# Last three products of the first pair's first conditional layer taken at two levels, and the fourth mW1 unit expanded later

## The chip, the cores and the metric

The kernel runs on one core of one Trainium2 chip. The metric is device microseconds of one execution. Before the change the median of three runs is 1162.1 us (1162.05, 1162.10 and 1163.01). All times below are microseconds from the start of the profiled execution's span unless they are said to be durations.

## What is computed

Four sequences of 512 tokens by 512 channels pass an attention with a projection, then two feed-forward networks, then a small adapter:

```
attn_out = softmax(x Wq (x Wk)^T * scale) x Wv Wp + bp
cms      = gelu(attn_out cW1 + cb1) cW2 + cb2 + one_hot(code)
modifier = gelu([attn_out, cms] mW1 + mb1) mW2 + mb2
y        = clip(x + cms + modifier, 0, 1)
out      = layernorm(y + gelu(y Wdown[s] + bd) Wup[s] + bu) * g + b
```

cW1 is 512 x 2048, cW2 2048 x 512, mW1 1024 x 2048, mW2 2048 x 512; everything is float32. The change lies in the first line of the feed-forward part, `gelu(attn_out cW1 + cb1)`, and in the preparation of mW1.

## The kernel before

**Pairs and layers.** The four sequences are worked on as two pairs; in a pair one sequence gives the left and the other the right column block of the right-hand operand. After the attention of both pairs, the loop over pairs runs five stages: `c1_layer` (cW1 and gelu), `second_layer` with cW2 (called c2 below), `m1_layer` (mW1 and gelu), `second_layer` with mW2 (m2), and the adapter, which for the first pair is spread over the second pair's c1.

**Seven products for eight, at one or two levels.** Every layer is a Strassen-Winograd product: seven block products numbered 1 to 7 stand for eight. In c2, m1 and m2 each of the seven is again cut into seven (two levels). In c1 of the second pair all seven products are at two levels (`c1_two_level`). In c1 of the first pair only products 1 and 5 are; products 2, 6, 7, 3 and 4 are plain products of 128x512 matmuls (L1327). The order is `FIRST_C = (2, 1, 5, 6, 7, 3, 4)`.

**What a two-level product of c1 needs.** It needs the four sums of its weight block (five to eight in the weight tile, operands of inner products 5, 6, 7 and 3) and the four sums of its token block. The weight sums of products 6, 7, 3 and 4 (`C1_BESIDE`) are made on GpSimd in the weight tile itself (L1229: 8 instructions of 128x256 for a product, for two weight tiles). The token sums are made by `inner_sums` (L1168 on): by VectorE, or on GpSimd with four 128x256 instructions (L1176 to L1179). `seven` runs the inner products in the order 1, 5, 6, 2, 7, 3, 4: the first uses unsummed blocks, the second needs the first weight sum and the first token sum. When product 6 or 7 is at two levels, its results are added into the hidden blocks partly by GpSimd (L1267: eight 128x512 additions for a product).

**Weight tiles.** Four tiles `wslot` are used in turn, two for a product, loaded by SP in a fixed order (`fetch`). A product's tiles come free when the product two before it has ended.

**Expansion.** Ahead of c2, m1 and m2 the weights are expanded on GpSimd: `expand` takes one unit (256 columns or rows of each block), makes seven sets of sums and writes them to DRAM (`m1_kept` and so on), from where SP loads them as they are needed. `expansion` is a generator: two units of cW1, two of cW2, then the four units of mW1. `steps` advances it between pieces of the attention and after each piece of the first pair's c1. A unit first issues its sums, three plain sets, the raw load of the next unit (`then`, four DMAs at L381), three full sets, and last the `fourth` set, which is written into the tiles `first` and `part`. `late_expansion` does the same for the two units of mW2 during m1, in the tiles `mod`, `slot[0]`, `slot[6:8]`.

**What sets the order.** The order in which each engine issues its instructions is fixed when the program is built: a planner goes by program order among the instructions that it believes ready at its own estimate of the time. `tc.keep_in_program_order(i)` pins an instruction behind the one traced before it on its engine. Once built, an engine takes its queue strictly in order: one that waits holds up all behind it.

**The step into c2.** `second_operands` prepares the operands of c2 and m2 from the hidden blocks: `operands(0)` are the four sums of the block `h22` for the first product of the second layer (product 3 in `SECOND`), `differences` the outer operands, and `after(p, g)` is called when a part of c1 or m1 is done. For the first pair's c1 (`busy`) VectorE makes `operands(0)` and half of two differences while product 4 runs; for the second pair's c1 GpSimd makes `operands(0)`, and half of the first difference is made by a scaled copy on ScalarE (L1448) and an adding DMA (L1455).

Of the kernel before, what the change touches and what calls it, by code (L numbers as in the profile page):

```python
# [18 lines left out]
def kernel(  # L19
# [121 lines left out]
    def flat(t):  # L141
        return t.rearrange("p c n -> p (c n)")
# [117 lines left out]
    C1_PLAIN = {1: (0, 0), 2: (1, 0), 4: (1, 1)}  # L260
    C1_SUM = {3: 2, 6: 0, 7: 1}
    C1_BESIDE = (6, 7, 3, 4)
    C1_KEPT = (2,)

    c1_outer = [spill.tile([P, 3, 2, 2, 256], F32, name=f"c1_outer{u}") for u in range(2)]
# [188 lines left out]
    def expansion():  # L454

        c2_units = [(cW2, False, c2_kept, u) for u in range(2)]
        yield from expand_c1(0, lambda: load_c1(1, nc.gpsimd))
        yield from expand_c1(1, lambda: load_raw(cW2, False, 0, slot[4:6]))

        constants()  # L460
        yield from expand_all(
            c2_units + m1_units, slot[4:6], (flat(part), slot[3], slot[1]), flat(first)
        )

    def late_expansion():

        spaces = (flat(mod[0]), flat(mod[1]), slot[0])
        quarters = lambda tiles: [t[:, at : at + 1024] for t in tiles for at in (0, 1024)]
        begin, rest = expand_c1_late(quarters(slot[6:8]), quarters(spaces[:2]))
        yield from expand_all(m2_units, slot[6:8], spaces, None, begin)  # L470
        yield from rest

    def inner_weights(src, is_first, store, p, u):

# [685 lines left out]
    def c1_operands(slots=(0, 1, 2, 3)):  # L1160


        at0, at1, t12, t34 = (in_rows[i] for i in slots)
        b11, b12, b21, b22 = at0[:, 0:2, :], at1[:, 0:2, :], at0[:, 2:4, :], at1[:, 2:4, :]
        t1, t2, t3, t4 = t12[:, 0:2, :], t12[:, 2:4, :], t34[:, 0:2, :], t34[:, 2:4, :]
        operands = {1: b11, 2: b21, 3: b22, 4: t4, 5: t1, 6: t2, 7: t3}

        def inner_sums(p, k, eng=None):  # L1168

            s = mod[1][:, 2 * k : 2 * k + 2, :].rearrange("p a (b n) -> p (a b) n", b=2)  # L1170
            t = operands[p]
            s1, s2, s3, s4 = (s[:, i : i + 1, :] for i in range(4))
            if eng is None:
                return inner_operands(t, 1, [s1, s2, s3, s4], pinned=True)
            c11, c12, c21, c22 = t[:, :1, :256], t[:, :1, 256:], t[:, 1:, :256], t[:, 1:, 256:]
            eng.tensor_tensor(s1, c12, c11, ALU.subtract)  # L1176
            eng.tensor_tensor(s2, c22, s1, ALU.subtract)
            eng.tensor_tensor(s3, c22, c12, ALU.subtract)
            eng.tensor_tensor(s4, c21, s2, ALU.subtract)  # L1179
            return {1: c11, 2: c21, 3: c22, 4: s4, 5: s1, 6: s2, 7: s3}  # L1180

        def minus(out_, one, two):
            tc.keep_in_program_order(nc.vector.tensor_tensor(out_, one, two, ALU.subtract))

        minus(t1, b12, b11)

        def rest():
            minus(t2, b22, t1)
            yield
            minus(t3, b22, b12)  # L1190
            minus(t4, b21, t2)
            yield

        return operands, inner_sums, rest()
# [2 lines left out]

        tc.keep_in_program_order(nc.sync.dma_start(out=out, in_=in_))

    def c1_two_level(p, h, rhs, after, beside):  # L1200


        a = []
# [64 lines left out]
            if p == 7 and place in ((0, 1), (1, 0)):  # L1268
                gelu(h[3], 1, cb1_c, (first_tile, first_tile + 1))

        then = {6: [beside], 7: [beside], 4: [beside]} if beside is not None and p != 2 else {}
        if p == 4:

            then[2] = [lambda: after(p, 0)]

        copy = nc.vector.tensor_copy if p in (3, 4) else nc.scalar.copy
        seven(2, matmuls, keep, (1, 5, 6, 2, 7, 3, 4), then, copy, at=mod[0])
        if p == 5:
            gelu(h[0], 0, cb1_c, range(8))
        elif p == 6 and 3 in C1_BESIDE:  # L1280
            after(3, 0)
        elif p in (3, 4):
            after(p, 1)

    def c1_layer(h, rhs, after, more, beside):

        operands, inner_sums, rest = rhs
        two = [p for p in FIRST_C if p in ((2, 1, 5, 6, 7, 3, 4) if more else (1, 5))]
        ready = {}

        def prepare(i):
# [5 lines left out]
        for p in FIRST_C:  # L1297
            if p in two:
                if more or p == 1:
                    prepare(two.index(p) + 1)  # L1300
                c1_two_level(p, h, ready[p], after, beside if more else None)
                if more:
                    next(rest, None)
                yield
                continue
            for g in range(2):
# [27 lines left out]
                        combine_first_tile(p, h, 4 * g + t, ps, cb1_c)  # L1334
                if p == 2:
                    next(rest, None)
                after(p, g)
                if more:
                    beside()
                yield  # L1340

    def combine_first_tile(p, h, t, ps, bias_c):
        h11, h12, h21, h22 = (b[:, t, :] for b in h)
        if p == 6:
            add(ps, ps, h21)
            add(h12, ps, h22)
            nc.scalar.copy(h21, ps)
        elif p == 7:
            add(ps, ps, h21)
            add(h22, ps, h22)  # L1350
            nc.scalar.copy(h21, ps)
            gelu(h[3], 1, bias_c, (t,))
        else:
            i, half = {3: (1, 0), 4: (2, 1)}[p]
            dst = h[i][:, t, :]
            add(dst, ps, dst)
            gelu(h[i], half, bias_c, (t,))

    def m1_operands():

# [56 lines left out]

    LOW, HIGH = slice(0, 4), slice(4, 8)

    def second_operands(h, busy=False, eng=None):  # L1420

# [17 lines left out]
        def after(p, g):  # L1441

            if (p, g) == (3, 1) and eng is not None:
                ready.append(operands(0, eng))
            if (p, g) == (3, 0) and not busy:
                for two in (slice(0, 2), slice(2, 4)):
                    tc.keep_in_program_order(
                        nc.scalar.activation(t1[:, two, :], h11[:, two, :], AF.Copy, scale=-1.0)  # L1448
                    )
            elif (p, g) == (3, 1):  # L1450
                if busy:
                    differences(1, LOW)
                    differences(3, LOW)
                else:
                    nc.gpsimd.dma_start(out=t1[:, LOW, :], in_=h12[:, LOW, :], accum_op=ALU.add)  # L1455
            elif (p, g) == (4, 0) and eng is None:
                ready.append(operands(0))
            elif (p, g) == (4, 1):
                differences(1, HIGH)

        def begin():
            if not busy:
                differences(3, LOW)

        ready = []
        return operands, differences, after, ready, begin

    def second_layer(made, src, kept_w, c, last, bias_c, beside):

        operands, differences, _, ready, begin = made  # L1470
        c11, c12, c21, c22 = c
# [1 line left out]
        for i, p in enumerate(SECOND):  # L1473
# [19 lines left out]
            def matmuls(q, ps):  # L1493
# [14 lines left out]
            inner(  # L1508
                matmuls, [[v[:, o, t, :] for t in range(2)] for o in range(2)], 256,
                None if half is None or bias_c is None else bias_c[:, half : half + 2],  # L1510
                first if bias_c is not None else mod[0],
            )
            if p == 6:
                z6 = z
# [217 lines left out]
    for pair in range(B // 2):  # L1732
        final = pair == B // 2 - 1

        h = next_hidden()
        made = second_operands(h, pair == 0, nc.gpsimd if final else None)
        between = expanding if pair == 0 else extra
        for _ in c1_layer(h, c1_rhs, made[2], final, lambda: steps(extra, 1)):
            if not final:
# [4 lines left out]
        m1_made = m1_operands()  # L1744
        m1_rhs = []

        def beside_c2(i, pair=pair):
            if i == 4:

                load_attn(pair)  # L1750
            elif i == 6:
                m1_rhs.append(m1_made(0))

        for _ in second_layer(made, cW2, c2_kept, blocks_of(cms), c_last(pair), None, beside_c2):
            pass

        h = next_hidden()
        made = second_operands(h)
# [118 lines left out]
```

## Time and profile before

| | |
|---|---|
| median of 3 runs | 1162.1 us |
| profiled execution: its own time | 1163.66 us |
| its span, first to last instruction | 1162.0 us |
| granted TensorE clock | 0.999 |
| PE / DVE / ACT / POOL busy | 99% / 77% / 25% / 46% of the span |
| first pair: c1 | 237.43 to 330.27 |
| first pair: c2 | 330.27 to 415.08 |
| first pair: m1 | 415.08 to 585.37 |
| first pair: m2 | 585.37 to 669.98 |

PE is TensorE, DVE VectorE, ACT ScalarE, POOL GpSimd, SP the queue that issues the weight loads. A line of the timeline view gives start, duration, engine, source line, operation, output and input, and in brackets how long the engine sat idle before it and what ended that wait. The chain of waits names the work that led to the end of the program, followed back step by step.

### The profile page before, as it was taken

The numbers are of one execution on the slowest core, as the hardware profiler recorded it, in microseconds if no ns is written. First come the engines' busy times: TensorE is split into PE (matmuls) and PEld (weight loads), VectorE is DVE, ScalarE is ACT, GpSimd is POOL, SyncE is SP. The second block draws the span as 40 slices with busy tenths as digits, with TensorE's granted clock in tenths as the row PEclk, the third lists the DMA queues.
The fourth block names the chain that finished last, engine by engine and source line by source line (L and its number), as shares of the span: only waits on it lengthen the run. The fifth ranks groups of instructions, "written<-read, shape, count | busy, mean of one in ns | idle before, by whom it ended". The sixth has DMA issues, their size and how long they took to land.

```text
span 1162.0 us, 13643 instructions
## 1 busy us (share of the span) xinstructions
PE 1153.4 (99%) x4941; PEld 922.6 (79%) x4941; DVE 892.2 (77%) x1227; ACT 293.5 (25%) x535; POOL 532.4 (46%) x611
## 2 busy tenths in 40 slices
PE   9999999999999999999999999999999999999997
PEld 8588468556478888888888877778888888888875
DVE  5755755487699965899699956789994588689955
ACT  4244426235520000013310036372000003230014
POOL 4999989888950068795200317971000001120001
PEclk9999999999999999999999999999999999999999
DMA  9695594898676578888837742145745364585601
GB/s 278 252 268 188 190 399 172 320 368 289 263 271 239 182 249 317 321 285 334 263 130 305 224 158 91 65 161 197 267 156 188 146 240 158 177 304 193 230 3 72
DMA packets 100482, 258.87 MB, mean 223 GB/s; under 512 B 23554, under 2 KB 58688, under 8 KB 85184
## 3 DMA queue, kind: packets, MB, share of 16 engines
q1 hardware_dynamic: 77088, 157.17, 38.5%
q0 software_dynamic: 19888, 89.17, 21.6%
q10 hardware_dynamic: 3440, 11.67, 2.6%
q8 instruction: 39, 0.64, 0.2%
q14 instruction: 27, 0.22, 0.1%
HBM read 188.78 MB, written 66.06 MB: 219 GB/s over the span
## 4 chain that ended last, share of the span: by engine, by line
PE 97%; DVE 2%; issue 1%; DVEq 0%
PE i L1495 29%; PE i L1395 27%; PE sum L756 10%; PE sum L1237 9%; PE sum L690 8%; PE c L1327 6%; PE down_ps L1587 2%; PE up_ps L1606 2%; PE tr_ps L522 1%; DVE hidden L600 1%; PE up_ps L1601 1%; DVE slot L252 1%; DVE part L1099 0%; PE tr_ps L943 0%; PE idle_ps L237 0%
## 5 line engine op out<-in xcount | busy, mean ns | idle before, releaser
L1395 PE MATMUL i<-slot,wslot 128*128 128x256 f32 x1184 | 261.4, 379 | 0.6 <-DVE part L1099 0.6
L1395 PEld LDWEIGHTS i<-slot,wslot 128*128 128x128 f32 x1184 | 224.6, 190 | 32.1 <-DVE part L1099 1.3
L1495 PE MATMUL i<-slot,wslot 128*128 128x256 f32 x896 | 202.7, 379 | 0.0
L1495 PEld LDWEIGHTS i<-slot,wslot 128*128 128x128 f32 x896 | 170.2, 190 | 23.4 <-DVE cms L1099 0.3
L1495 PE MATMUL i<-hidden,wslot 128*128 128x256 f32 x576 | 132.1, 379 | 0.0
L1495 PEld LDWEIGHTS i<-hidden,wslot 128*128 128x128 f32 x576 | 109.4, 190 | 15.7 <-issue 0.7
L1099 DVE TENSOR_TENSOR part<-i,part 128x512 f32<-128x512 f32 (+1 forms) x156 | 90.5, 591 | 34.0 <-PE i L1395 24.6
L1106 ACT COPY first<-i 128x512 f32<-128x512 f32 (+1 forms) x42 | 21.6, 514 | 375.7 <-PE i L1395 220.9
L1128 ACT ACTIVATE hidden<-hidden,bias 128x512 f32<-128x512 f32 x128 | 83.9, 716 | 87.3 <-DVE hidden L600 77.3
L1763 POOL DMA_DIRECT2D slot<-xT_kept x4 | 2.8, 706 | 152.9 <-PE i L1395 152.9
L1237 PE MATMUL sum<-mod,wslot 128*128 128x256 f32 x288 | 66.6, 379 | 0.0
L252 DVE TENSOR_TENSOR slot<-hidden 128x1024 f32<-128x1024 f32 x46 | 61.4, 1334 | 0.0
L1237 PEld LDWEIGHTS sum<-mod,wslot 128*128 128x128 f32 x288 | 54.7, 190 | 7.4
L1766 POOL TENSOR_TENSOR cms<-cms,slot 128x512 f32<-128x512 f32 x16 | 26.0, 1650 | 73.2 <-PE i L1395 42.6
L252 DVE TENSOR_TENSOR slot<-hidden,slot 128x1024 f32<-128x1024 f32 x46 | 56.7, 1234 | 0.3
L1327 PE MATMUL c<-slot,wslot 128*128 128x512 f32 x128 | 55.3, 592 | 0.0
L1099 DVE TENSOR_TENSOR part<-i,first 128x512 f32<-128x512 f32 (+1 forms) x50 | 31.4, 632 | 29.4 <-PE i L1395 18.5
L600 DVE TENSOR_TENSOR sum<-sum,wslot 128x512 f32<-128x512 f32 x48 | 33.2, 696 | 26.3 <-PE sum L756 18.6
L600 DVE TENSOR_TENSOR hidden<-part,hidden 128x2048 f32<-128x2048 f32 x20 | 52.9, 2646 | 0.5
L756 PE MATMUL sum<-hidden,wslot 128*128 128x256 f32 x232 | 53.2, 379 | 0.0
L381 POOL DMA_DIRECT2D slot<-in_L_cond_mW x24 | 17.9, 752 | 73.3 <-DVE slot L252 72.3
L1327 PEld LDWEIGHTS c<-slot,wslot 128*128 128x128 f32 x128 | 24.3, 190 | 30.6 <-issue 27.7
(344 smaller groups left out, 2097.1 us busy)
## 6 DMA issues: line engine op xcount, KB each, us to landing
wslot<-m_kept SPq DMA_DIRECT2D x48, 1024.0 KB, 6.4
wslot<-m_kept SPq DMA_DIRECT2D x36, 512.0 KB, 4.5
wslot<-c_kept SPq DMA_DIRECT2D x16, 1024.0 KB, 6.3
slot<-in_L_cond_mW POOLq DMA_DIRECT2D x24, 512.0 KB, 7.4
wslot<-in_L_cond_mW SPq DMA_DIRECT2D x24, 512.0 KB, 6.3
wslot<-in_L_cond_cW SPq DMA_DIRECT2D x40, 256.0 KB, 5.0
slot<-in_L_cond_cW POOLq DMA_DIRECT2D x12, 512.0 KB, 6.2
m_kept<-wide POOLq DMA_DIRECT2D x6, 1024.0 KB, 7.5
```

The lines of the kernel that those rows point to most:

```text
L252: i = eng.tensor_tensor(out_, one, two, ALU.subtract)
L600: nc.vector.tensor_tensor(dst, a, b, ALU.add)
L690: nc.tensor.matmul(ps, lhsT=lhs[p][:, c, r * P : (r + 1) * P], rhs=rhs[p][:, c, :], start=(first_ and c == 0), stop=(c == 1), skip_group_c ...
L756: nc.tensor.matmul(v[:, j, :], lhsT=lhs[p][:, c, j * P : (j + 1) * P], rhs=rhs[p][:, c, :], start=(first_ and j == 0 and c == 0), stop=(c ...
L1099: nc.vector.tensor_tensor(dst, ps, other, ALU.add)
L1128: nc.scalar.activation(block[:, t, :], block[:, t, :], AF.Gelu, bias=bias_c[:, 8 * half + t : 8 * half + t + 1],)
L1237: nc.tensor.matmul(halves_of(ps)[:, j, :], lhsT=a[g][:, at_[q], j * P : (j + 1) * P], rhs=rhs[q][:, 0, :], start=(first_ and j == 0), stop ...
L1327: nc.tensor.matmul(ps, lhsT=lhs(c, t), rhs=operands[p][:, c, :], start=(c == 0), stop=(c == 1),)
L1395: nc.tensor.matmul(out_ps[:, j, :], lhsT=a[j][q][:, c, :], rhs=now[q][:, c, :], start=(c == 0), stop=(c == 1),)
L1495: nc.tensor.matmul(ps[:, :256], lhsT=a[k // 2][q][:, k % 2, :], rhs=now[q][:, k, :], start=(k == 0), stop=(k == 3),)
L1587: nc.tensor.matmul(ps, lhsT=wd[:, c, n * P : (n + 1) * P], rhs=y[:, c, tokens], start=(c == 0), stop=(c == NV - 1),)
L1766: nc.gpsimd.tensor_tensor(cms[s][:, d, :], cms[s][:, d, :], in_rows[3][:, d, :], ALU.add)
```

## The change

- In the first pair's c1, products 7, 3 and 4 also go through `c1_two_level` (`C1_TWO`). Their weight sums come on GpSimd, as those of the second pair do.
- Their token sums are made on GpSimd, all twelve instructions pinned one behind the other, traced right behind product 5. The ones of 7 and 3 lie in `mod[1]`, those of 4 in `first`.
- `expansion` ends with the third unit of mW1. The fourth is made by `expand_in_place` in two parts: its raw load is issued at the second product of c2 into `mod`; one set (of block a11) is made at the seventh product of c2 in the tile of `h[2]`; all others follow when c2 is done, in the tiles of `h[2]` and `h[0]`, and a11, a21 and a12 are overwritten by their own sums.
- The first pair's step into c2 is made as the second pair's: `operands(0)` on GpSimd, half of the first difference by ScalarE and an adding DMA, half of the third at c2's start. The call `after(3, 0)` comes behind product 7 for the first pair.
- The first pair's c2 uses `first` in place of `mod[0]` for its intermediate.

```diff
+    AHEAD = (7, 6)
+    C1_TWO = ((1, 5, 7, 3, 4), (2, 1, 5, 6, 7, 3, 4))
...
-            c2_units + m1_units, slot[4:6], (flat(part), slot[3], slot[1]), flat(first)
+            c2_units + m1_units[:3], slot[4:6], (flat(part), slot[3], slot[1]), flat(first)
...
+    def expand_in_place(space, later):
+        u = 3
+        load_raw(mW1, True, u, [flat(t) for t in mod])
+        yield
...
+        def keep(p, a, to, sums_too=True):
+            inner_sums(a, to)
+            at = m1_kept[p, u]
+            if sums_too:
+                nc.gpsimd.dma_start(out=block(at[:, :1024]), in_=a)
+                at = at[:, 1024:]
+            nc.gpsimd.dma_start(out=at, in_=to)
+
+        keep(1, a11, spaces[0], False)
+        yield
+        s1 = block(spaces[4])
+        nc.gpsimd.tensor_tensor(s1, a21, a22, ALU.add)
+        inner_sums(s1, spaces[5])
+        nc.gpsimd.dma_start(out=m1_kept[5, u], in_=later[:, :2048])
+        nc.gpsimd.tensor_tensor(a21, a11, a21, ALU.subtract)
+        nc.gpsimd.tensor_tensor(a11, s1, a11, ALU.subtract)
+        keep(6, a11, spaces[6])
+        keep(7, a21, spaces[7])
+        keep(2, a12, spaces[1], False)
+        nc.gpsimd.tensor_tensor(a12, a12, a11, ALU.subtract)
+        keep(3, a12, spaces[2])
+        keep(4, a22, spaces[3], False)
+        yield
...
-        def inner_sums(p, k, eng=None):
-            s = mod[1][:, 2 * k : 2 * k + 2, :].rearrange("p a (b n) -> p (a b) n", b=2)
+        def inner_sums(p, k, eng=None, fixed=False):
+            space = first if k == 2 else mod[1][:, 2 * k : 2 * k + 2, :]
+            s = space.rearrange("p a (b n) -> p (a b) n", b=2)
...
+            for out_, one, two in ((s1, c12, c11), (s2, c22, s1), (s3, c22, c12), (s4, c21, s2)):
+                i = eng.tensor_tensor(out_, one, two, ALU.subtract)
+                if fixed:
+                    tc.keep_in_program_order(i)
...
-        two = [p for p in FIRST_C if p in ((2, 1, 5, 6, 7, 3, 4) if more else (1, 5))]
+        two = [p for p in FIRST_C if p in C1_TWO[more]]
...
+                c1_two_level(p, h, ready[p], after, then)
+                if p == 5 and not more:
+                    for k, later in enumerate((7, 3, 4)):
+                        ready[later] = inner_sums(later, k, nc.gpsimd, True)
+                if p == AHEAD[more]:
+                    after(3, 0)
...
-        made = second_operands(h, pair == 0, nc.gpsimd if final else None)
+        made = second_operands(h, nc.gpsimd)
...
+        last_unit = iter(()) if final else expand_in_place(flat(h[2]), flat(h[0]))
+
+        def beside_c2(i, pair=pair, last_unit=last_unit):
+            if i in (1, 6):
+                next(last_unit, None)
...
-        for _ in second_layer(made, cW2, c2_kept, blocks_of(cms), c_last(pair), None, beside_c2):
+        for _ in second_layer(
+            made, cW2, c2_kept, blocks_of(cms), c_last(pair), None, beside_c2,
+            mod[0] if final else first,
+        ):
             pass
+        next(last_unit, None)
```

## The prediction

> **What bounds the kernel.** I read the page's first part, the chain of waits, the busy time by stage over the first pair's c1, and then GpSimd's timeline there.
>
> ```profile
> PE 1153.4 (99%) x4941; PEld 922.6 (79%) x4941; DVE 892.2 (77%) x1227; ACT 293.5 (25%) x535; POOL 532.4 (46%) x611
> ...
> 237.43 13.73 PE c L1327 x32
> 251.16 24.17 PE sum L1237 x112
> 275.34 54.93 PE c L1327 x128
> 330.27 84.81 PE i L1495 x392
> 415.08 60.45 PE i L1395 x280
> ```
>
> TensorE never rests, and through c1 the chain is TensorE alone. So a matmul that goes is time that goes, and a wait that comes is time that comes. The fourth line is products 6, 7, 3 and 4, plain: 54.93 / 4 = 13.73 each. The third is products 1 and 5 at two levels: 24.17 / 2 = 12.09 each.
>
> ```profile
> 275.30:289.10 13.80, 13.80 (x34) 6.14 (x33) 10.45 (x15) 4.81 (x9) 9.63 (x15) 1.00 1.02 361
> 289.10:302.80 13.70, 13.70 (x33) 6.05 (x32) 11.12 (x16) 8.33 (x15) 12.25 (x12) 1.00 0.84 334
> 302.80:316.50 13.70, 13.70 (x34) 6.05 (x33) 6.23 (x9) 7.26 (x11) 13.63 (x19) 1.00 0.63 230
> 316.50:330.30 13.80, 13.80 (x34) 6.14 (x33) 13.72 (x10) 3.62 (x6) 13.73 (x15) 1.00 0.78 295
> ```
>
> One line is one product (6, 7, 3, 4); the columns are stretch and length, then PE, PEld, DVE, ACT and POOL (each with its count), clock, DMA share, GB/s. POOL is what to look at: GpSimd, which is to make the new sums, is already full here, with units three and four of mW1.
>
> ```profile
> 272.51 3.01 POOL L381 DMA_DIRECT2D slot<-in_L_cond_mW  x4
> ...
> 279.63 0.57 POOL L398 DMA_DIRECT2D m_kept<-part  x1
> ...
> 284.25 0.73 POOL L247 TENSOR_TENSOR slot<-slot 128x256 f32<-128x256 f32 x1
> 290.52 0.73 POOL L242 TENSOR_TENSOR part<-first 128x256 f32<-128x256 f32 x1 [5.54 <-DMA m_kept<-part]
> ...
> 294.94 2.38 POOL L395 TENSOR_TENSOR part<-slot,slot 128x1024 f32<-128x1024 f32 x1
> ```
>
> Here unit three ends: the raw load for unit four, the full sets up to 284.98, a wait until the store of `part` has landed, the fourth set, and at 294.94 unit four begins.
>
> **What goes.** Three products at 13.73 - 12.09 = 1.64 us: 4.9 us of TensorE, all on the path. Product 7 still begins at 289.0, since nothing ahead of it changes on TensorE.
>
> **When GpSimd gets to the new work.** The token sums are pinned behind unit three, so its end counts. The raw load (3.01) goes, so the full sets end at 281.97 and the store of `part` is issued at 276.6. Before, it took 10.9 us from issue to its release (279.63 to 290.5), with 2 MB of raw load ahead; the same store issued at 197.74 had landed by 203.07, at most 5.3 us. I take 6, nearer the second row since the load is gone: landing at 282.6. The fourth set lasts 4.4 us (290.52 to 294.92), so unit three ends at 287.0; with the two rows as bounds, 286.4 to 291.9.
>
> [...]
>
> **What GpSimd then has to do.** Prices come from the second pair's c1, where all of these exist:
>
> ```profile
> 741.74 5.77 POOL L1229 TENSOR_TENSOR wslot<-wslot 128x256 f32<-128x256 f32 x8
> ...
> 752.11 4.95 POOL L1267 TENSOR_TENSOR hidden<-hidden,hidden 128x512 f32<-128x512 f32 x4
> ...
> 778.21 2.38 POOL L252 TENSOR_TENSOR slot<-hidden 128x1024 f32<-128x1024 f32 x1
> ```
>
> Weight sums: 5.77 for a product. Additions of product 7: 4.95 / 4 = 1.24, eight are 9.9. `operands(0)`: starts 2.33 apart, four are 9.7 (with their last one's tail). Token sums: 128x256 instructions start 0.69 apart in unit three, twelve are 8.3. Together 3 x 5.77 + 9.9 + 9.7 + 8.3 = 45.2 us, beginning at 287.0; the three products and c2's first product want it by about 330. The second pair has 115.7 us for its c1 (669.98 to 785.68), with adapters in between; here four products have some 50.
>
> **Product 7.** Inner product 1 runs to 289.0 + 1.73 = 290.7. Inner product 5 needs the first weight sum. Those sums stand behind the twelve token sums in program order, and the token sums are ready at once when unit three ends. So I put the weight sums behind all twelve: 287.0 + 8.3 = 295.3, the first done at 296.0. Wait: 5.3 us. After that each later weight sum comes 1.4 us apart for a pair and inner products last 1.73, so nothing more. Bounds: nothing, if the planner slots the weight sums between or ahead of the token sums (their tiles are loaded by about 283); 10.2, if unit three ends at 291.9.
>
> [...]
>
> **Products 3 and 4.** Product 7 ends at 289.0 + 12.09 + 5.3 = 306.4. GpSimd: weight sums of 7 to 301.1, of 3 (tiles free since 289.0) to 306.8. Product 3 needs the first at 308.1: no wait. The additions follow to 316.7. Then `operands(0)`, traced ahead of product 4's weight sums, competes with them. Its third and fourth sums overwrite `slot[7]`, which product 3 still reads, so I put two of the four first (4.7), then the weight sums: the first done at 322.1. Product 4 starts at 318.5 and needs it at 320.2: 1.9 us. Bounds: nothing, if the weight sums go first; 6.9, if all four go first (316.7 + 9.7 + 0.7 - 320.2). c1 ends at 318.5 + 12.09 + 1.9 = 332.5, 2.2 later than the 330.27 of before. The last sums of `operands(0)` end near 332, and c2's inner product 7 needs the third at 332.5 + 5.2: covered.
>
> **VectorE, ScalarE and SP.** Product 7 costs VectorE 16 instructions of 0.69 as before (two by eight tiles). Products 3 and 4 rise from 8 to 18 of 0.65 to 0.70, some 12 of 12.09 us: covered, but barely. The pieces that leave it (`operands(0)`, 325.46 to 334.42, and the 3.76 at 317.18) come off the same stretch. In the second pair, with the same work, c2 took 84.61 (785.68 to 870.29), so I carry 0, up to 1 us if the cover fails. SP loads the same bytes; c2's first tiles come free at product 3's end and the loads take 6.3, a product ahead.
>
> **The fourth unit.** Four raw issues (3.01) and one set (2.8 and 0.57) fall in c2, where GpSimd is idle from 334.5 to 406.7 and VectorE busy 11.9 of 12.1; one set cannot cost more than its 3.4, and I take nothing. After c2 there follow 4 x 2.35 + 24 x 0.69 + 9 x 0.57 = 31 us, and behind that the mW2 expansion: it reuses `mod`, so it starts near 447 and not 410.95, and ends near 560 (533.70 before, its first 10 us of raw waits gone). Its first stores for m2 fall at some 545, against m2's start at 585: in time. Behind it queue the xT load and the cms additions (7.8 and 7.1: until 575) and the adding DMA of L1455 (9.2 to landing: 585), wanted some 12 us into m2. In time. What I do charge: in 487.6 to 512.2 VectorE is busy 24.32 of 24.6 and TensorE loses 0.6, with VectorE's 128x512 sums stretched from 0.68 to 3.31 beside GpSimd. The overlap moves into 536 to 585, where VectorE has 20 and 19 of 24.4. First pair's m1 is 170.29, the second's 169.37, so at most 0.9 can be won; I take 1.0 lost, bounds -0.9 and 3.
>
> **Sum.** -4.9 + 5.3 + 1.9 + 0 + 1.0 = +3.3 (the 0.1 is rounding of 4.93). The profiled execution was 1163.66 with a span of 1162.0, so 1.6 above the median of 1162.1; I add the difference to the median: **1165.3 us**.
>
> **Rivals.**
> 1. *The weight sums come early* (faster). The planner issues product 7's weight sums before or between the token sums. For it: in the second pair GpSimd's weight and token sums are interleaved (703 to 713). Against it: there each token sum waited for its space, here nothing holds them. Product 7 then waits 0 to 1, product 4 nothing to 1.9: -4.9 + 0.5 + 0.5 + 0.8 = -3.1, 1159.0. It decides when the first weight sum is done before 293.3, which leaves a wait of 2.6 in all.
> 2. *GpSimd's lateness and the saving cancel*: unit three ends at 286.4 (wait 4.7), product 4's weight sums go first, m1 as before: -0.2 to +2, near 1162.8.
> 3. *`operands(0)` as a whole ahead of product 4's sums*, and unit three nearer its late bound: waits 7.5 and 6.9, +10.5, 1172.
> 4. *The saving is not there*, as two-level products need VectorE for 18 instructions: +1 a product. It is within the others' range.
>
> **Chances.** Forecast (two waits, 1164.5 to 1168.5) 0.40; rival 1 0.22; rival 2 0.23; rival 3 0.15. Faster by over 0.2% (2.3 us, about what a measurement of this kernel can tell from no change) is rival 1: 0.22. Within 0.2%: rival 2 and no more, 0.23. Slower: 0.55. Range: 1159.2 to 1171, which leaves out half of rival 1 and the worst of 3; the likeliest case's own is 1164.5 to 1168.5.
>
> **What would show it.** L1237 in place of L1327 for products 7, 3 and 4, 12.1 us each but for waits; a TensorE wait near 290.7 that a GpSimd L1229 ends, of 5 us; a second near 320; unit three's end near 287; m1's length against 170.29. Wrong if the first L1229 comes ahead of the pinned token sums, or if the largest wait lies with VectorE or in m2.

## The result, and the profile after

The changed kernel takes **1177.8 us** (median of four runs, 1175.74 to 1179.21), against 1162.55 for the kernel before on the same chip: a ratio of 1.0129, with a 95% interval of 1.011 to 1.0149. It is slower, and above the range of the prediction.

The profiled execution took 1179.05 us, its span 1177.3, so 15.3 more than the 1162.0 of before. By the starts of each stage's first matmul in TensorE's timeline, the first pair's stages went so: c1 from 92.84 to 97.32, c2 from 84.81 to 85.58, m1 from 170.29 to 180.97, m2 84.60 and 84.61. The rest of the kernel gave 0.6 back. So m1, whose own products the change leaves as they were, lost most.

First the page's line of busy time, then the stretches of products 6, 7, 3 and 4 (columns as in the prediction):

```profile
PE 1153.3 (98%) x5013; PEld 938.5 (80%) x5013; DVE 911.5 (77%) x1242; ACT 291.8 (25%) x531; POOL 582.1 (49%) x662
```

```profile
275.10:288.75 13.65, 13.65 (x34) 6.00 (x33) 10.44 (x15) 4.68 (x8) 12.18 (x19) 1.00 0.97 379
288.75:310.26 21.51, 15.22 (x58) 12.18 (x56) 9.64 (x15) 2.25 (x4) 21.04 (x29) 0.84 0.19 66
310.26:322.35 12.09, 12.09 (x58) 10.64 (x57) 11.35 (x19) 5.64 (x9) 10.57 (x10) 1.00 0.22 66
322.35:334.43 12.08, 12.08 (x57) 10.64 (x56) 11.27 (x19) 7.74 (x13) 12.06 (x11) 1.00 0.80 270
```

Products 3 and 4 take 12.09 as priced. Product 7 takes 21.51, 9.4 too many. TensorE's timeline there, then GpSimd's (idle time and what ended it in brackets):

```profile
288.75 1.89 PE L1274 MATMUL sum<-slot,wslot 128*128 128x256 f32 x8
296.15 2.08 PE L1274 MATMUL sum<-mod,wslot 128*128 128x256 f32 x4 [5.52 <-POOL wslot L1266]
299.01 4.51 PE L1274 MATMUL sum<-mod,wslot 128*128 128x256 f32 x12 [0.78 <-POOL wslot L1266]
```

```profile
286.24 0.53 POOL L415 DMA_DIRECT2D m_kept<-part  x1
286.79 0.74 POOL L1214 TENSOR_TENSOR mod<-slot 128x256 f32<-128x256 f32 x1
...
295.38 11.48 POOL L1266 TENSOR_TENSOR wslot<-wslot 128x256 f32<-128x256 f32 x16
306.81 7.43 POOL L1304 TENSOR_TENSOR hidden<-hidden,hidden 128x512 f32<-128x512 f32 x6
315.76 2.37 POOL L252 TENSOR_TENSOR slot<-hidden 128x1024 f32<-128x1024 f32 x1 [1.51 <-ACT hidden L1164]
...
320.54 5.57 POOL L1266 TENSOR_TENSOR wslot<-wslot 128x256 f32<-128x256 f32 x8
```

The queue is the predicted one: unit three ends at 286.79, twelve token sums, then the weight sums from 295.38. The wait is 6.3 us in two pieces: the first ends with the first weight sum, the second with the fifth, at 299.01. But x4 and x12 matmuls take 2.08 and 4.51 us where they take 1.1 and 2.9 at full clock (e_filled below); the stretches behind the wait show why, by the clock in the third column from the end:

```profile
296.00:298.00 2.00, 1.85 (x4) 1.18 (x4) 0.00 (x0) 0.00 (x0) 1.92 (x4) 0.50 0.03 8
298.00:300.00 2.00, 1.22 (x3) 0.84 (x3) 0.69 (x1) 0.00 (x0) 2.00 (x4) 0.50 0.00 0
300.00:303.00 3.00, 3.00 (x10) 2.46 (x9) 1.00 (x2) 0.00 (x0) 2.92 (x5) 0.60 0.00 0
```

At the border of c2 and m1 the two stretches of 24 us before m1 differ in one engine, of before and of after:

```profile
391.10:415.10 24.00, 24.00 (x113) 21.13 (x112) 23.86 (x36) 0.75 (x2) 4.70 (x5) 1.00 0.60 194
```

```profile
396.00:420.00 24.00, 24.00 (x113) 21.12 (x112) 23.83 (x26) 0.75 (x2) 22.53 (x20) 1.00 0.61 216
```

GpSimd is busy 22.53 instead of 4.70; VectorE is busy as long as before, but gets 26 instructions done and not 36. GpSimd's first piece of unit four there, and the sum `s1` of its second part, 7.2 us before c2 ends at 420.01:

```profile
396.58 0.72 POOL L242 TENSOR_TENSOR hidden<-mod 128x256 f32<-128x256 f32 x1 [59.34 <-DVE cms L1135]
...
412.77 2.37 POOL L496 TENSOR_TENSOR hidden<-mod,mod 128x1024 f32<-128x1024 f32 x1
```

VectorE's timeline in the changed kernel, and then one of the same sums before:

```profile
416.76 0.41 DVE L1135 TENSOR_TENSOR part<-i,part 128x256 f32<-128x256 f32 x1
...
419.03 2.83 DVE L252 TENSOR_TENSOR slot<-slot,slot 128x512 f32<-128x512 f32 x1
421.79 1.21 DVE L252 TENSOR_TENSOR slot<-slot 128x512 f32<-128x512 f32 x1
422.92 2.83 DVE L252 TENSOR_TENSOR slot<-slot,slot 128x512 f32<-128x512 f32 x1
```

```profile
407.13 0.68 DVE L252 TENSOR_TENSOR slot<-slot,slot 128x512 f32<-128x512 f32 x1
```

The three 128x512 sums took 0.68 each before. The addition that reads TensorE's result (`i`, in PSUM, the memory that TensorE writes) keeps its 0.41. TensorE pays for the late sums of m1's first product:

```profile
429.02 5.22 PE L1431 MATMUL i<-slot,wslot 128*128 128x256 f32 x16 [5.39 <-DVE part L1135]
```

Those x16 took 3.62 elsewhere: again a low clock, 0.50 in the 3 us behind the wait. A second wait, 2.92 us at 532.13, has the clock at 1.00 behind it and follows one late addition. VectorE, then GpSimd:

```profile
519.71 0.68 DVE L1135 TENSOR_TENSOR part<-i,first 128x512 f32<-128x512 f32 x1
520.32 8.45 DVE L252 TENSOR_TENSOR slot<-cms,slot 128x512 f32<-128x512 f32 x1
528.69 0.68 DVE L1135 TENSOR_TENSOR part<-i,part 128x512 f32<-128x512 f32 x1
```

```profile
520.13 2.37 POOL L397 TENSOR_TENSOR mod<-mod,slot 128x1024 f32<-128x1024 f32 x1
...
527.50 0.72 POOL L245 TENSOR_TENSOR wide<-wide,slot 128x256 f32<-128x256 f32 x1
528.16 0.80 POOL L414 DMA_DIRECT2D m_kept<-slot  x1
```

From 520.13 GpSimd goes from one operation between SBUF tiles to the next without a gap; VectorE's sum, with both operands in SBUF (the on-chip memory of the tiles), ends at 528.77, while GpSimd issues a DMA.

The 8.45 us is far more than the longest GpSimd instruction of that stretch (2.37): the sum lasts through seven of them. What holds it there the trace does not show; it shows the 8.45 us and where they end, and above the 2.83 of sums between SBUF tiles and the 0.41 of an addition that reads PSUM.

### The profile page after: what moved, and what is told of

The parts are those of the page before. It is cut to its first block, busy times and chain, and to the rows that moved or that the text cites. A ratio compares the mean times of both kernels' runs of the same rounds, so it can differ in the third digit from the quotient of the medians.

```text
span 1177.3 us, 13921 instructions
## 1 busy us (share of the span) xinstructions
PE 1153.3 (98%) x5013; PEld 938.5 (80%) x5013; DVE 911.5 (77%) x1242; ACT 291.8 (25%) x531; POOL 582.1 (49%) x662
## 4 chain that ended last, share of the span: by engine, by line
PE 87%; DVE 6%; DMA 3%; POOL 2%; issue 2%; SPq 0%; DVEq 0%; POOLq 0%
PE i L1431 25%; PE i L1526 24%; PE sum L1274 11%; PE sum L792 10%; PE sum L726 8%; DVE slot L252 3%; PE down_ps L1618 2%; PE up_ps L1637 2%; PE c L1369 2%; DMA wslot<-in_L_cond_mW 1%; DMA wide<-hidden 1%; PE tr_ps L558 1%; DVE part L1135 1%; DVE hidden L1451 1%; DMA wide<-in_L_cond_Wq 1%
## 5 line engine op out<-in xcount | busy, mean ns | idle before, releaser
L1142 ACT COPY first<-i 128x512 f32<-128x512 f32 (+1 forms) x49 | 24.2, 494 | 456.3 <-PE i L1431 242.6
L1526 PEld LDWEIGHTS i<-hidden,wslot 128*128 128x128 f32 x576 | 109.4, 190 | 15.3 <-issue 0.5
L1274 PE MATMUL sum<-mod,wslot 128*128 128x256 f32 x352 | 84.3, 388 | 6.3 <-POOL wslot L1266 6.3
L1274 PEld LDWEIGHTS sum<-mod,wslot 128*128 128x128 f32 x352 | 68.4, 195 | 17.0 <-POOL wslot L1266 7.4
L636 DVE TENSOR_TENSOR hidden<-sum,hidden 128x512 f32<-128x512 f32 x74 | 48.7, 685 | 16.7 <-ACT hidden L1292 9.3
L636 DVE TENSOR_TENSOR sum<-sum,mod 128x512 f32<-128x512 f32 x72 | 48.9, 695 | 13.1 <-PE sum L1274 12.2
L252 DVE TENSOR_TENSOR slot<-hidden 128x1024 f32<-128x1024 f32 x44 | 57.9, 1316 | 0.0
L1135 DVE TENSOR_TENSOR part<-i,first 128x512 f32<-128x512 f32 (+1 forms) x56 | 33.8, 609 | 24.3 <-PE i L1431 13.7
L636 DVE TENSOR_TENSOR hidden<-part,hidden 128x2048 f32<-128x2048 f32 x20 | 50.5, 2526 | 0.5
L792 PEld LDWEIGHTS sum<-hidden,wslot 128*128 128x128 f32 x232 | 43.8, 190 | 5.8
```

The costliest lines, as they stand in the source:

```text
L252: i = eng.tensor_tensor(out_, one, two, ALU.subtract)
L636: nc.vector.tensor_tensor(dst, a, b, ALU.add)
L792: nc.tensor.matmul(v[:, j, :], lhsT=lhs[p][:, c, j * P : (j + 1) * P], rhs=rhs[p][:, c, :], start=(first_ and j == 0 and c == 0), stop=(c ...
L1135: nc.vector.tensor_tensor(dst, ps, other, ALU.add)
L1142: nc.scalar.copy(c1, p1)
L1274: nc.tensor.matmul(halves_of(ps)[:, j, :], lhsT=a[g][:, at_[q], j * P : (j + 1) * P], rhs=rhs[q][:, 0, :], start=(first_ and j == 0), stop ...
```

## The experiments

Times are medians of the runs, with lowest and highest; the ratio is to the kernel before on the same chip, with its 95% interval; c1, c2 and m1 are those of the profiled execution. Executions of most variants differ by several us among themselves, where the kernel before keeps within some 3, but for one run of 1169.24.

| kernel | us | ratio | c1 | c2 | m1 |
|---|---|---|---|---|---|
| before | 1162.55 (1162.05–1163.24) | | 92.84 | 84.81 | 170.29 |
| changed | 1177.83 (1175.74–1179.21) | 1.0129 [1.011, 1.0149] | 97.32 | 85.58 | 180.97 |
| e_hold | 1171.70 (1169.64–1175.33) | 1.008 [1.0067, 1.0093] | 97.62 | 84.78 | 172.92 |
| e_vector | 1175.78 (1174.32–1179.87) | 1.0122 [1.0107, 1.0136] | 96.33 | 84.61 | 176.98 |
| e_both | 1169.72 (1167.84–1170.21) | 1.0052 [1.0039, 1.0065] | 96.09 | 84.61 | 174.29 |
| e_plain | 1173.74 (1171.25–1176.54) | 1.009 [1.0077, 1.0104] | 92.84 | 84.61 | 180.76 |
| e_sums | 1170.30 (1168.49–1175.11) | 1.0071 [1.0056, 1.0086] | 91.42 | 84.61 | 176.58 |
| e_filled | 1180.59 (1178.10–1185.97) | 1.0141 [1.0126, 1.0156] | 96.08 | 88.69 | 185.67 |
| e_behind | 1176.51 (1176.43–1178.56) | 1.0119 [1.0105, 1.0134] | 95.43 | 86.70 | 177.51 |
| e_none | 1167.47 (1165.52–1169.30) | 1.004 [1.0025, 1.0055] | 96.99 | 84.61 | 169.43 |
| e_late | 1175.71 (1168.41–1178.81) | 1.0111 [1.0096, 1.0127] | 97.39 | 85.20 | 170.67 |
| e_mixed_hold | 1165.63 (1163.87–1170.35) | 1.0024 [1.0012, 1.0035] | 91.29 | 86.73 | 172.30 |
| e_mixed_late | 1164.88 (1162.14–1176.67) | 1.0033 [1.0008, 1.0058] | 90.39 | 86.52 | 171.20 |
| e_queue | 1165.83 (1162.96–1171.66) | 1.0026 [1.0011, 1.0042] | 90.89 | 84.61 | 175.17 |
| e_copy | 1173.38 (1170.25–1176.47) | 1.0091 [1.0076, 1.0106] | 97.75 | 84.61 | 172.59 |
| e_all | 1175.58 (1173.03–1179.29) | 1.0098 [1.0084, 1.0113] | 99.44 | 84.60 | 178.78 |
| e_all_late | 1169.76 (1168.83–1171.29) | 1.0059 [1.0046, 1.0072] | 98.80 | 84.61 | 170.39 |
| e_last | 1163.78 (1161.12–1168.37) | 1.0007 [0.9992, 1.0022] | 89.86 | 84.61 | 172.31 |
| e_last_late | 1160.78 (1159.28–1165.77) | 0.9987 [0.9976, 0.9999] | 89.39 | 84.61 | 170.47 |

### m1: unit four's place

**e_hold**

```diff
+        held = nc.gpsimd.tensor_tensor(s1, a21, a22, ALU.add)
+        with tc.issue_after(held.ins):
+            ...
```

> The changed kernel with one edit: the part two of mW1 unit four is issued on GpSimd only behind its own sum s1, which needs the last feature-block of the third product's gelu and so cannot run before c2 ends. Of unit four only the first set (about 7 us of GpSimd) is left in c2's tail; in the changed kernel some 23 us of it stood there. Theory A (VectorE's instructions are stretched beside GpSimd's in c2's tail, so that m1's first operand sums come late): TensorE's wait of 5.39 us at m1's start and the 1.6 us at a low clock behind it go, nearly whole: 1179 - 7 = 1172 us, m1 near 174 us; VectorE's 128x512 adds in c2's last 24 us are near 0.7 to 1.0 us again. Rival B (VectorE is late because the transfer of unit four's raw weights held its adding transfer in c2, and because c1 ended late): the wait stays at 4 us or more, 1177 to 1180 us. Rival C (the work held back now stands in m1's first products instead and costs there what it cost before): 1176 to 1182 us with waits of TensorE for VectorE in products 2 to 4 of m1. c1 is to keep its 97.2 us in each.

1171.70, m1 172.92: theory A. Two points were wrong. VectorE's 128x512 sums are not all near 0.7 to 1.0 again: one at 416.02 took 2.83. And `s1` did not wait for c2's end but began 11.0 us before it (7.2 in the changed kernel, where other sets had already gone ahead). GpSimd was busy 16.3 of c2's last 24 us, not 22.5, and two waits of 1.48 and 1.07 us stayed.

**e_none**: `last_unit = iter(())` and, in `inner_weights`, `u = min(u, 2)`. It leaves the expansion of unit four out and takes unit three's sets in its place.

> The changed kernel without the expansion of mW1's unit four at all (this kernel leaves that part of the computation out: none of its GpSimd work, raw loads and stores; the first m layer of the first pair takes unit three's sets in its place, at the same loads). GpSimd then stands idle in all of c2. Theory A (all that m1 loses against its 170.3 us of before comes of GpSimd's work on unit four in c2's tail, and of the late expansion pushed back behind it): the waits of 5.4 and 2.9 us for VectorE and the low clock go, no add of VectorE between operands in the SBUF is over 1.3 us for 512 columns in c2's last 25 us, m1 is at 169.4 to 170.5 us, c2 at 84.6 us, and the whole at 1178 - 10.7 - 0.8 = 1166.5 us, c1 keeping its 97.2 us. Rival B (m1's loss comes of the later end of c1, or of the changed order of the queues): m1 stays at 174 us or more.

m1 169.43, c2 84.61, 1167.47, within 1 us of theory A; no wait of TensorE over 0.5 us is left in m1. The stretch of 24.3 us before m1, and the sums in it, are like those of before again:

```profile
394.00:418.30 24.30, 24.30 (x115) 21.38 (x114) 23.40 (x34) 0.74 (x2) 4.95 (x6) 1.00 0.59 198
```

```profile
408.53 0.68 DVE L252 TENSOR_TENSOR slot<-slot,slot 128x512 f32<-128x512 f32 x1
```

So all of m1's loss, and c2's, comes with unit four's work and what it pushes back.

**e_late**: part two behind a GpSimd copy of one column of `in_rows[2]`, traced inside m1.

> The changed kernel with the part two of mW1's unit four held back further than in the run with the hold: behind VectorE's sum for m1's second product (by a GpSimd copy of one column of it, 128x1), so that it starts behind m1's start, where the earlier hold still let it start 11 us before c2's end. Only the first set (5 us of GpSimd) is left in c2's tail. Theory A (contention of GpSimd with VectorE's sums at the border is the whole of the loss there): the two waits left with the earlier hold (1.48 and 1.07 us) go too, m1 is at 170 to 171 us where the hold had 172.9, the whole 2 us below the hold's 1171.7: 1169.5 us. Rival B (what is held back costs the same later: the late expansion is pushed back by some 13 us more, towards m1's end): waits for loads or for VectorE's sums of 2 to 6 us at m1's last products, 1171 to 1176 us.

The edit did less than meant. The sum it waits for was made long before m1 (the copy ran 11.4 us before m1's start), so `s1` moved only from 11.0 to 8.0 us ahead of m1. The profiled m1 was 170.67, yet the median is 4 us above e_hold's and the executions spread over 10 us. The run does not tell the two theories apart.

### c1: who makes the sums, and in which order

**e_plain**: `C1_TWO = ((1, 5), ...)`, the rest of the change kept.

> The changed kernel with products 7, 3 and 4 of the first pair's first layer at one level again, as before the change; everything else of the change stays (unit four's expansion in two parts late, operands of the last products by GpSimd, the adding transfer later). So none of the twelve token sums and of the 24 weight sums is made. Theory A (c1's loss comes from the three products, m1's from unit four's place, each by itself): c1's first pair is 92.8 us again, m1 keeps 179 to 182 us: 1179 - 4.3 = 1174.7 us. Rival B (m1's loss is a late consequence of c1's): m1 is near 171 us, 1163 to 1166 us.

Theory A: c1 92.84, m1 180.76 (1.80 us of it a wait for a weight load), 1173.74. m1's loss does not need c1's: TensorE waits 4.73 us at m1's start here too. c2's 0.8 is not there.

**e_vector**

```diff
                 if p == 5 and not more:
+                    ready[7] = inner_sums(7, 0)
+                ...
```

> The changed kernel with one edit: the token sums of products 7, 3 and 4 of the first pair's first layer are made by VectorE (product 7's ahead of product 5, 3's behind 5, 4's behind 7), not by GpSimd. GpSimd then makes product 7's weight sums directly behind unit three. Theory A (product 7 waited only because its weight sums stood behind twelve token sums): the waits of 5.52 and 0.78 us in product 7 go, and with them the 2.95 us at half clock: c1's first pair 97.2 - 9.3 = 88 us, the whole 1179 - 9.3 = 1169.5 us. Rival B (VectorE cannot carry twelve sums more beside GpSimd in c1): its additions for c1's outputs are late, TensorE waits for it in products 5 to 3, 1173 to 1179 us. Rival C (the weight sums wait for something else, the buffers of unit three or product 5's readers): the waits in product 7 stay at 3 us or more. m1 keeps its 181 us in A and B.

Rival B. Product 7 no longer waits, but c1 gains 1 us only. The wait stands in product 5 now: 5.14 us for VectorE. Ahead of it stands again one sum with two SBUF operands, which ends (at 272.23) as GpSimd has issued a DMA. VectorE, then GpSimd:

```profile
267.43 4.80 DVE L252 TENSOR_TENSOR mod<-slot,mod 128x256 f32<-128x256 f32 x1
```

```profile
269.22 2.35 POOL L397 TENSOR_TENSOR first<-slot,slot 128x1024 f32<-128x1024 f32 x1
271.52 0.57 POOL L400 DMA_DIRECT2D m_kept<-slot  x1
```

**e_both**: both edits.

> The two edits together: token sums of products 7, 3 and 4 by VectorE, and part two of unit four issued behind its sum s1. If the two losses are independent (one in c1, GpSimd's order; one at the border of c2 and m1, contention), their gains add: 1179 - 9.3 - 7 = 1163 us, and what is left over the 1157 us that the removed 4.9 us alone would give is m1's later wait (2.9 us), m1's end (1 us) and c2's 0.8 us. Rival: they are not independent (the earlier end of c1 gives VectorE its lead back, so that the hold adds nothing): 1166 to 1170 us, the same as one of the two alone.

1169.72. By the number this is the rival's range. But it is 2 us below e_hold, and the gains of e_hold (6.1) and e_vector (2.1) add up to 8.2 where 8.1 was measured, as independent losses would; the forecast of 1163 carried e_vector's too large gain. With executions that spread over 2.4 to 5.7 us this run alone does not decide between them; that m1's loss stands without c1's is shown by e_plain.

**e_sums**: the token sums of 7 and 3 behind product 5, those of 4 behind 7, all on VectorE; and a second profile of the same kernel (e_sums_hold in the record; no hold is in it).

> As the kernel with the token sums by VectorE, but product 7's and product 3's token sums stand behind product 5 in VectorE's order (not product 7's ahead of it), and product 4's behind product 7. There, an add of VectorE whose two operands lie in the SBUF took 4.8 us beside GpSimd's unit three (0.42 us alone), the additions from PSUM behind it in the queue came late, and TensorE waited 5.14 us in product 5. Theory A (that add, caught beside GpSimd, was the whole loss; GpSimd's order is the whole of product 7's wait): no wait of TensorE over 0.5 us in the first pair's first layer, no slice of it at a low clock: 92.84 - 4.94 = 87.9 us for it, against 97.2 in the changed kernel and 96.3 in the last one. The whole: 1178 - 9.4 = 1168.5 us, if m1 keeps its 177 to 181 us. Rival B (VectorE cannot carry twelve additions more there at all, wherever they stand): waits of 3 us and more for VectorE in product 7 or 3, c1 at 92 to 97 us.

> A second look at the kernel just before this one, for the spread of the waits between two executions of one kernel: c1 within 0.3 us of the first look, m1 within 4 us.

c1 91.42 and 91.89, not 87.9: neither theory as put. Product 7's wait for GpSimd is gone; the eight sums on VectorE beside unit three took 9.8 us (0.42 each alone), the additions behind them came late, and c1 lost 3.5 us to waits of 0.70 and less. The second look: m1 176.18, 1168.91.

**e_behind**: only product 7's token sums ahead of its weight sums.

> The changed kernel with GpSimd's order in the first layer altered and nothing moved to another engine: behind unit three come product 7's four token sums, then its eight weight sums, and only then the eight token sums of products 3 and 4 and the other weight sums. [...] c1: 88 to 93 us, the whole 1169 to 1174 us. Rival B (GpSimd's sum of work between unit three and product 4 is the bound, not its order): c1 stays at 95 us or more, the wait standing at product 4.

Rival B, by c1 of 95.43. GpSimd's first weight sum now lets TensorE go on at 291.35, where in the changed kernel it stood in the queue behind eight more token sums and let TensorE go on at 296.15 only. Product 7 still waited 0.56 and 1.72 us and product 4 then 2.96. From unit three's end to product 4's first weight sum GpSimd has 12 x 0.69 + 11.5 + 9.9 + 2.4 = 32 us of work in its queue, and TensorE without a wait leaves it some 28: an order within that only moves the wait.

**e_filled**

```diff
+                        for _ in range(24):
+                            tc.keep_in_program_order(nc.tensor.matmul(
+                                spare[:, :P], lhsT=zeros, rhs=zeros, start=True, stop=True
+                            ))
```

> The changed kernel with 24 products of zeros (128x128, into a bank that nobody reads) in TensorE's order between the first of product 7's sums and its second, where TensorE waits 5.5 us for GpSimd's weight sums. They keep TensorE at work for some 3 to 7 us of that wait and change nothing else. Theory A (the wait itself costs 6.3 us, and the idle time costs 2.95 us more because TensorE's granted clock falls to a half for the 5 us behind it): the clock in the 7 us behind the wait is 1.00 and not 0.5 to 0.6, product 7 takes 21.5 - 2.95 = 18.5 us, the whole is 2.9 us below the changed kernel: 1175 to 1176 us. Rival B (the low clock comes from something else, as the load on the chip): the clock stays at 0.5 to 0.6 there and the time at 1178 us.

The clock stayed at 1.00: the low clock does come from the idle time. TensorE's timeline (a product shows as two records), and one of its stretches:

```profile
290.46 5.52 PE L1342 MATMUL spare<-zeros 128*128 128x128 f32 x48
296.56 1.13 PE L1274 MATMUL sum<-mod,wslot 128*128 128x256 f32 x4 [0.58 <-POOL wslot L1266]
299.40 2.86 PE L1274 MATMUL sum<-mod,wslot 128*128 128x256 f32 x12 [1.71 <-POOL wslot L1266]
```

```profile
298.00:300.00 2.00, 0.60 (x3) 0.55 (x4) 0.48 (x1) 0.00 (x0) 2.00 (x4) 1.00 0.00 0
```

But product 7 took 20.27 us (288.73 to 309.00), 1.2 less and not 2.95: at full clock TensorE runs into GpSimd's next sum, and the second wait grows from 0.78 to 1.71. The whole was no faster, with longer waits in c2 and m1 in the profiled execution (2.09, 4.75 and 4.75 us for VectorE). The shortest of the three, in c2, has slow matmuls behind it as well (x16 in 5.41 us where the next x16 take 3.62):

```profile
363.09 5.41 PE L1535 MATMUL i<-slot,wslot 128*128 128x256 f32 x16 [2.09 <-DVE cms L1135]
```

### What is left, and a version that is faster

**e_mixed_hold** and **e_mixed_late**: product 7's token sums by VectorE behind product 5, product 3's by GpSimd behind product 7's weight sums, product 4's by VectorE behind product 7; the two holds.

> Three edits together, towards a version that is faster than both: product 7's token sums by VectorE behind product 5, product 3's by GpSimd behind product 7's weight sums, product 4's by VectorE behind product 7; and part two of unit four behind its sum s1. VectorE has only four sums ahead of its additions from PSUM where it had eight (e_sums lost 3.5 us to that), GpSimd has four token sums where the changed kernel has twelve. If both mechanisms hold: c1 at 88 to 89.5 us, c2 84.7, m1 172.5 to 174.5: 1163 - 4.4 + 3.2 = 1161.5 us. If GpSimd's product 4 sums now come late: up to 2 us in c1, 1163.5 us.

> The kernel just before this one with the further hold in place of the hold (unit four's part two behind VectorE's sum for m1's second product). c1 as in that kernel; m1 at 170 to 171 us if contention at the border is the whole: 1159 us; 1162 to 1166 us if the late expansion, pushed back, costs at m1's end what is gained at its start.

1165.63 and 1164.88. m1 is near the forecast; c1 kept 2.5 us and more (2.18 us for a copy of VectorE, behind product 4's sums), and c2 lost 1.9 and 1.7.

**e_queue**: `with tc.issue_after(adding[0].ins): load_raw(...)`.

> The last mixed kernel with the hold (product 7's and 4's token sums by VectorE, product 3's by GpSimd, part two of unit four held) and one edit more: the four raw loads of unit four are issued on GpSimd's queue behind the adding transfer of c2's operand, not two of them ahead of it. Theory A (c2's loss, 0.8 us in the changed kernel and 1.9 in that one, is the adding transfer sharing the engines with two raw loads issued ahead of it): VectorE's wait for it falls from 3 us to under 1 us, c2 is at 84.6 to 84.8 us against 86.7, the whole 2 us below 1165.6. Rival B (c2's loss comes of VectorE being late from c1): c2 stays above 86 us.

Theory A for c2: 84.61. The adding DMA was issued 1.9 us earlier and landed 1.9 us faster. VectorE's wait for the adding DMA, in e_mixed_hold and then here:

```profile
342.05 4.49 DVE L1461 TENSOR_TENSOR hidden<-hidden,hidden 128x2048 f32<-128x2048 f32 x2 [4.85 <-DMA wide<-hidden]
```

```profile
338.24 4.50 DVE L1464 TENSOR_TENSOR hidden<-hidden,hidden 128x2048 f32<-128x2048 f32 x2 [1.34 <-DMA wide<-hidden]
```

The median did not follow: m1 was 2.9 longer in the profiled execution, 2.60 of it a wait for a weight load at m1's end. Why that load is late stays open.

**e_copy**: product 3's copies on ScalarE.

> The same mixed kernel with the hold, and one edit more: product 3's two copies from PSUM (128x512) are made by ScalarE, not VectorE. In that kernel TensorE waited 2.18 us for such a copy, which stood behind product 4's token sums in VectorE's order. Theory A (VectorE's order in c1 is what is left of c1's loss): that wait goes, c1 falls from 91.3 to 88.5 to 89.5 us, the whole from 1165.6 to 1163.5. Rival B (VectorE is simply full, 4.00 of 4 us in those slices): another addition from PSUM is late in place of the copy, c1 at 90.5 us or more.

Rival B by the number (c1 97.75), but not by its cause: TensorE waited 4.98 us for ScalarE, whose copies stood behind gelus that waited for GpSimd's additions, and then 2.54 for VectorE.

**e_all** and **e_all_late** carry that copy too and show no more than it (4.27 and 4.36 us for ScalarE).

> The two edits of the runs before it together, with the hold: c1 88.5 to 89.5, c2 84.7, m1 172.3: 1165.6 - 2 - 2 = 1161.5 us, 0.1 per cent below the kernel before the change, if both hold; 1163.5 if one does.

> The same with the further hold of unit four's part two (behind VectorE's sum for m1's second product): m1 at 171 us in its best executions, 1160 us; but the kernel with that hold had executions 10 us above its best, where the pushed-back late expansion ran into m1's last products, so that a median of 1161 to 1165 us would show that the loss is moved and not removed.

**e_last** and **e_last_late**: e_queue with product 4's token sums in the middle of product 3, and c2's four operand sums behind product 4's weight sums.

```diff
+                    then = {2: [fourth_sums]}
...
+        made = second_operands(h, nc.gpsimd, (4, 0) if pair == 0 else (3, 1))
```

> The kernel with the adding transfer first (e_queue) and two edits in c1: product 4's token sums by VectorE in the middle of product 3, behind that product's copies from PSUM and not ahead of them; and the four operand sums of c2's first product by GpSimd behind product 4's weight sums, not one of them ahead. In that kernel TensorE waited 1.78 and 0.67 us for VectorE there. If VectorE's order was what was left of c1's loss, c1 is at 88 to 88.5 us (it was 90.9), c2 at 84.6 to 84.8, m1 at 172 to 175: 1165.8 - 2.5 = 1163.3 us, as before the change within 0.1 per cent. If the operand sums are now late for c2's first product: a wait for GpSimd of 1 to 3 us there in exchange.

> The same with the further hold of unit four's part two: m1 at 170.4 to 171.2 us in its best executions, 1160.5 us as best; the median 1161 to 1165 us, if part of the executions runs into the late expansion at m1's end as in the other kernels with that hold.

1163.78 and **1160.78**; the second is faster than the kernel before by a ratio of 0.9987 (0.9976 to 0.9999). That is the only one of seventeen edited kernels below 1, and its interval just leaves 1 out, so a gain of 0.1% is likely and not certain. c1 stayed some 1 us above its forecast in both (89.86, 89.39). In e_last_late TensorE's waits of over 0.5 us in the first pair's c1, c2 and m1 are two:

```profile
313.58 1.13 PE L1281 MATMUL sum<-mod,wslot 128*128 128x256 f32 x4 [1.23 <-DVE sum L641]
417.47 1.99 PE L1449 MATMUL i<-slot,wslot 128*128 128x256 f32 x8 [0.89 <-DVE part L1140]
```

Of the 4.9 us of removed products 3.45 remain in c1 (92.84 - 89.39). The two kernels differ in the hold alone, and `s1` begins 11.0 and 8.3 us ahead of m1; since the same pair of holds went the other way between e_hold and e_late, what the 3 us between them come from stays open.

## Why the prediction was wrong

- **The saving** (-4.9): right. Products 3 and 4 take 12.09. (The sum itself, 1162.1 + 3.3, is 1165.4 and not 1165.3.)
- **Product 7's wait** (5.3): right in place and cause, 1.0 short (6.3). Unit three's end was 286.79 for 287.0. 0.78 of it is the second piece, which the prediction had ruled out ("so nothing more").
- **Left out: the clock behind the wait.** 2.95 us in the profile; e_filled shows that idle time makes it, and that only 1.2 can be had back there, since GpSimd is next. Five long waits in the first pair's stages have slow matmuls behind them: 5.52 and 5.39 us in the changed kernel (clock 0.50), 4.98 in e_copy (x8 in 3.78 us, 1.89 elsewhere), 4.73 in e_plain (x16 in 5.49, 3.62 elsewhere) and 4.36 in e_all_late (x8 in 3.57). The short ones differ: behind 2.96 (e_behind, x16 in 3.72), 2.92 (changed kernel, clock 1.00) and 2.54 (e_copy, x8 in 1.99) the matmuls kept their time, and behind 2.75 (e_all_late, x8 in 3.08), 2.09 (e_filled, c2) and 1.72 (e_behind, x12 in 4.34 for 2.86, with a wait of 0.56 just ahead) they did not. So no length measured here separates the two. The prediction priced the wait without it.
- **Product 4's wait** (1.9): 0. The weight sums went ahead of all but one of `operands(0)`, and the late product 7 gave them time.
- **VectorE, SP, c2** (0, up to 1): 0.77. VectorE waited 3.01 us for the adding DMA, which landed 12.1 us after its issue with two raw loads ahead of it; e_queue shows that order to be the cause in the mixed kernel.
- **The fourth unit** (+1.0, bounds -0.9 and 3): 10.7, and this is the step that failed. I wrote "one set cannot cost more than its 3.4, I take nothing" and "After c2 there follow [...] 31 us". The trace order of the kernel does not hold the rest back: what needs only the tile of `h[2]`, and even `s1` in that of `h[0]`, went ahead of c2's end, and GpSimd was busy 22.5 of c2's last 24 us. There VectorE has no slack (busy 23.83 of 24 us) and works between SBUF tiles. I had read the price from 487.6 to 512.2 (0.68 stretched to 3.31) and applied it to m1's later part only. Of the 10.7, 7.0 stand at m1's first product (5.39 and the slow matmuls behind it) and 2.9 at 532.13, in the later overlap for which I had the 1.0. e_none (169.43), e_hold (172.92) and the changed kernel (180.97) follow GpSimd's busy time in those 24 us: 4.9, 16.3 and 22.5. The other kernels without a hold, at 22.5 too, have m1 between 176.2 and 185.7; those with one, at 16 to 18, between 170.4 and 172.9, but for three with a late weight load at m1's end.
- Together: 3.3 + 9.7 + 1.0 + 2.95 - 1.9 + 0.8 - 0.6 (elsewhere) = 15.25, against 15.3.
- **Rivals**: the first did not come; the weight sums stood behind all token sums. The second was right on product 4 and not on product 7's wait. The third put 1172 on the wrong waits. The fourth did not come, with 12.09 for products 3 and 4. None had a loss at c2's end.

## What to carry to other kernels

Before moving work to GpSimd or to another time on it, look at what VectorE does beside it: here additions that read PSUM kept their time (0.41), and sums between SBUF tiles took up to twelve times theirs (0.68 to 8.45), the four worst by that ratio until GpSimd issued a DMA (8.45 in the changed kernel, 8.41 in e_filled, 8.38 in e_plain, 4.80 for 0.42 in e_vector). Ask for a moved step when it can start at the earliest, not when it is traced. And price a wait of TensorE with the slow matmuls behind it (2.95 us in the changed kernel; behind each wait of 4.36 us and more listed above, and some of about 2), but count them only as far as the next thing that they would wait for.

## What the runs showed that was not expected

- A 128x512 sum of VectorE took up to 8.45 us (0.68 alone), a 128x2048 addition 9.83 in e_all_late (2.28 alone); the former, and the 4.80 us of a 128x256 sum in e_vector, ended with GpSimd's next DMA issue.
- GpSimd pays as well: its 128x256 operations took 1.17 us (at 513.86 in e_sums) and up to 2.77 (at 513.74 in the changed kernel) beside such sums, 0.72 alone.
- Executions of one kernel come to differ by 2 to 14 us (e_mixed_late: 1162.14 to 1176.67) where the kernel before keeps within some 3; which collisions differ was not traced, since each kernel left one profile, but for e_sums with two (c1 91.42 and 91.89, m1 176.58 and 176.18).
